# The second mixture of a two-layer perceiver: seven of eight tiles by blocks, one own block per expert

## The chip, the cores and the metric

The kernel runs on one core of a Trainium2 chip. The metric is the device time of one execution in microseconds (us). A core has five engines that run their own instruction streams in order: TensorE (PE, matrix products; its weight loads are listed as PEld), VectorE (DVE), ScalarE (ACT), GpSimd (POOL) and SyncE (SP, which only issues transfers here). Sixteen DMA engines move data between HBM and the on-chip memory. Everything is float32.

## The reference

Sixteen sequences of 64 tokens of width 256 (x, 1024 tokens, eight tiles of 128) and a context of 1601 rows per sequence pass two layers. Layer 0 has an attention with gathered samples, a self attention and a mixture of 8 experts. Layer 1 has a cross attention to the context, a state-space scan and a mixture of 32 experts. The last two parts are the ones that matter here:

```python
x = x + xattn1(layernorm(x), context)
x = x + attn1(layernorm(x))      # in projection, causal convolution of 4 taps, silu,
                                 # scan h = dA * h + dt * B * x over 16 states, gate, out projection
x = x + ffn1(layernorm(x))

def ffn1(x, ...):                                   # TOPK = 4, E = 32 experts, H = 128, HS = 512
    scores = softmax(flat @ router_w.T + router_bias)
    topk_scores, topk_idx = top_k(scores, TOPK)
    topk_scores = topk_scores / max(topk_scores.sum(-1), 1e-12)
    h = silu(einsum('nd,ehd->neh', flat, gate_w)) * einsum('nd,ehd->neh', flat, up_w)
    expert_out = einsum('neh,edh->ned', h, down_w)
    out = (take(expert_out, topk_idx) * topk_scores).sum(1)
    return out + silu(flat @ sgate_w.T) * (flat @ sup_w.T) @ sdown_w.T
```

Each token needs four of the 32 experts and all of the shared part, which is as large as four experts.

## The kernel before

PE, DVE and ACT follow an order that is written out by hand: Python generators yield between pieces of work, and a loop steps a main generator and a side generator in turn, so what is emitted first runs first on each of these engines. SP and POOL take their instructions in the order in which a scheduler places them, near the order of the program.

The cross attention (`Cross.step`) runs 128 steps, one for a sequence and a pair of heads, and three more that empty its pipeline. Since a tile is two sequences, tile t is complete after step 16(t + 1) + 3. While it runs, side work is stepped in it: layer 0's second half, and from step 56 on layer 1's state space (`Ssm.group`) and routing (`Route.group`) of the tiles that are complete. A group is two tiles. `Ssm.group` has a prelude (layer norm, input projection, convolution, step sizes), 16 scan steps over 128x512 elements (db, hs, hc on DVE, an add on POOL) and an output projection. `Route.group` writes a tile's mask, gates and normed rows (to `xnd` in HBM). Three groups run so; two tiles are left, whose sequences finish last.

After the third group comes `Table.slots`, still beside the cross attention. It turns the masks of six tiles into blocks of 128 rows, each for one expert: the tokens of each expert are counted and their counts rounded up to whole blocks, 6 * 128 * 4 slots and at most 127 rows of padding per expert, so 55 blocks at most (`NBA`). It computes each token's slot, each block's expert (`evr`) and each block's list of rows (`row`). The list is a sum of 48 small products (hb, hp) on PE, built in 8 parts of three tiles on DVE.

Then the cross attention's memory is given back, and the tail begins, in this order:

1. `dense(first, ...)`: the shared part of the six tiles, four parts of 128 hidden units, each in two chunks of 384 columns. Beside it `Ssm.group` of the last two tiles starts.
2. `sparse`: 55 blocks. `fetch` issues a block's gather of rows (POOL), reads its expert number into a register (SP) and loads that expert's weights (SP, 256 and 128 KB; 8 and 9 buffers, five blocks ahead). `turn` transposes the rows, `hidden` makes the hidden units, `down` the output, which ACT's queue writes to `ygd` in HBM two blocks at a time. Every second block steps the state space.
3. `dense(last, ...)`: the last two tiles, after their norm and routing, through the four shared parts and all 32 experts, each weighted by its gate, which is zero where the expert wasn't chosen. Every expert's weights are loaded again. Beside it `combine` gathers, for each of six tiles and four choices, the rows of `ygd` (24 gathers on POOL) and adds them to the residual with their gates.
4. The output of the last two tiles is stored.

Lines of the profile: L1040 is the cross attention's product with the context, L87 all plain products (told apart by their tiles: `st<-qf,cT` scores, `st<-xta,wg` shared parts, `st<-xbt,wg` blocks, `st<-gt,wg` the dense last tiles), L1026 the cross attention's output projection, L630 to L635 the table's parts, L1273, L1275 and L1280 the scan step on DVE, L1281 its add on POOL, L1298 and L1299 the swiglu, L1365 the blocks' gathers, L652 the gathers of `combine`.

Of the kernel before, what the change touches and what calls it, by code (L numbers as in the profile page):

```python
# [17 lines left out]
P = 128  # L18
# [31 lines left out]
NG = 4  # L50
# [3 lines left out]
NTA = NPAIR - TG  # L54
NBA = (NTA * P * TOP1 + E1 * (P - 1)) // P

# [8 lines left out]
def perceiver_kernel(ctx: ExitStack, tc: tile.TileContext, a: dict, out: bass.AP):  # L65
# [471 lines left out]
    def blocks_of(nt, ne, top):  # L537
        return (nt * P * top + ne * (P - 1)) // P
# [4 lines left out]
    xnd, ygd = mk(dram, [NTA * P, D], "xnd"), mk(dram, [blocks_of(NTA, E1, TOP1) * P, D], "ygd")  # L543

    class Table:


        def __init__(self, pool, nt, ne, top):
            self.pool, self.nt, self.ne, self.top = pool, nt, ne, top
            self.nb = blocks_of(nt, ne, top)  # L550
# [16 lines left out]
        def floor(self, y):  # L567
            sh = list(y.shape)
            yi, yf = mk(self.pool, sh, "fli", I32, bufs=1), mk(self.pool, sh, "flf", bufs=1)
            nc.vector.tensor_copy(yi, y)  # L570
            nc.vector.tensor_copy(yf, yi)
            nc.vector.tensor_tensor(y, yf, y, ALU.is_gt)
            nc.vector.tensor_tensor(y, yf, y, ALU.subtract)

        def slots(self):

            rp, on, nt, ne, nb, top = self.pool, self.on, self.nt, self.ne, self.nb, self.top
            n = nt * ne
            sh = [P, nt, ne]
# [4 lines left out]
            pos = mk(rp, sh, "pos", bufs=1)  # L584
            nc.vector.tensor_copy(pos.rearrange("p t e -> p (t e)"), pc)
            run_ = mk(rp, [P, nt + 1, ne], "run", bufs=1)
# [5 lines left out]
            own, end, base = (mk(rp, [P, ne], t, bufs=1) for t in ("nb", "end", "base"))  # L592
            nc.vector.tensor_scalar(own, run_[:, nt, :], float(P - 1), 1.0 / P, ALU.add, ALU.mult)
            self.floor(own)
            nc.vector.tensor_tensor_scan(end, on[:, :ne], own, 0.0, ALU.mult, ALU.add)
            nc.vector.tensor_tensor(base, end, own, ALU.subtract)
            nc.vector.scalar_tensor_tensor(pos, base.unsqueeze(1).to_broadcast(sh), float(P), pos, ALU.mult, ALU.add)
            sl, bk, self.w = (mk(rp, [P, top, nt], t, bufs=1) for t in ("slf", "bk", "gk"))
            tmp = mk(rp, sh, "tmp", bufs=1)
# [5 lines left out]
            tk, cf = mk(rp, [P, nt], "tokf", bufs=1), mk(rp, [P, P], "colf", bufs=1)  # L605
            nc.vector.tensor_copy(tk, self.tok)
            nc.vector.tensor_copy(cf, self.col)
            nc.vector.tensor_scalar(end, end, tk[:, :1], None, ALU.is_le)
            ev = mk(rp, [P, 1], "ev", bufs=1)
# [4 lines left out]
            nc.tensor.matmul(pe[:1, :nb], lhsT=ev[:nb], rhs=ident[:nb, :nb], start=True, stop=True)  # L614
# [3 lines left out]
            self.floor(bk)  # L618
            nc.vector.scalar_tensor_tensor(sl, bk, -float(P), sl, ALU.mult, ALU.add)
            self.expert = mk(rp, [1, nb], "evr", I32, bufs=1)  # L620
            nc.vector.tensor_copy(self.expert, pe[:1, :nb])
# [3 lines left out]
            half = nt // 2  # L625
            s1, s2 = [P, half, P], [P, half, nb]
            for q in range(2 * top):
                k, t = q // 2, slice(q % 2 * half, (q % 2 + 1) * half)
                hp, hb = mk(rp, s1, "hp", bufs=1), mk(rp, s2, "hb", bufs=1)
# [4 lines left out]
                for i in range(half):  # L634
                    nc.tensor.matmul(po, lhsT=hp[:, i, :], rhs=hb[:, i, :], start=q + i == 0, stop=q + i == 2 * top + half - 2)  # L635
# [531 lines left out]
    rows_d = [mk(dram, [NR, TOK], f"rows{g}") for g in range(NG)]  # L1167

    class Ssm:
# [15 lines left out]
        def group(self, g, wide=None):  # L1185
# [3 lines left out]
            tiles = range(g * TG, (g + 1) * TG)  # L1189
            sh = [P, KC, TOK]  # L1190
            xn = normed(tiles, "m", mp)
            yield
            xt = turned(xn, TG, "m", mp)
            yield
            xpad = mk(mp, [P, KC, NS2, S + NCONV - 1], "xpad")
            nc.gpsimd.memset(xpad[:, :, :, : NCONV - 1], 0.0)
            zs = mk(mp, sh, "zs")
            for e in range(2 * KC):
                pz = bank()[:, :TOK]
# [14 lines left out]
            pp = bank()[:NR, :TOK]  # L1214
            mm(pp, [(w_xp[:, c, :], xc[:, c, :]) for c in range(KC)])
            prm = mk(mp, [NR, TOK], "prm")
            nc.scalar.copy(prm, pp)
            nc.sync.dma_start(out=rows_d[g], in_=prm)

            def spread(r0, n, tag, bufs, pool=mp):  # L1220

                t = mk(pool, [P, n, TOK], tag, bufs=bufs)
                nc.sync.dma_start(out=t, in_=rows_d[g][r0 : r0 + n, :].unsqueeze(0).to_broadcast([P, n, TOK]))
                return t
# [63 lines left out]
            for t in range(TG):  # L1288
                po = bank()
                mm(po[:, :D], [(y[:, c, t * P : (t + 1) * P], w_out[:, c, :]) for c in range(KC)])  # L1290
                nc.vector.tensor_tensor(x4[:, g * TG + t, :], po[:, :D], x4[:, g * TG + t, :], ALU.add)
# [9 lines left out]
    class Route:  # L1301
        def __init__(self, rp, mp):
# [3 lines left out]
            self.tb = Table(rp, NTA, E1, TOP1)  # L1306
# [29 lines left out]
        def group(self, g):  # L1336
            xn = normed(range(g * TG, (g + 1) * TG), "m", self.mp)
            nc.sync.dma_start(out=xnd[g * TOK : (g + 1) * TOK, :].rearrange("(t p) d -> p t d", p=P), in_=xn)
            yield
            xt = self.xt[:, :, g * TOK : (g + 1) * TOK]  # L1340
            tp = transposes([xn[:, t, k * P : (k + 1) * P] for k in range(KC) for t in range(TG)])
            nc.scalar.copy(xt.rearrange("p k (t n) -> p k t n", n=P), tp.rearrange("p (k t) n -> p k t n", t=TG))
            yield
            for t in range(TG):
                j = g * TG + t
# [4 lines left out]
    def sparse(ep, tb):  # L1350

        AHEAD = 5
        xb, yb = {}, {}
        st = {}

        def fetch(i):

            if i >= tb.nb:
                return
            if i % 4 == 0:  # L1360
                m = min(4, tb.nb - i)
                st["ev"] = mk(ep, [1, 4], "ev4", I32, bufs=3)
                nc.vector.tensor_copy(st["ev"][:, :m], tb.expert[:, i : i + m])
            x = mk(ep, [P, D], "xb", bufs=6)
            nc.gpsimd.indirect_dma_start(  # L1365
                out=x, out_offset=None, in_=xnd, in_offset=bass.IndirectOffsetOnAxis(ap=tb.row[:, i : i + 1], axis=0)
            )
            v = nc.sync.value_load(st["ev"][0:1, i % 4 : i % 4 + 1], min_val=0, max_val=E1 - 1)
            wg = mk(ep, [P, KC, 2, HID1], "wg", bufs=8)
            wd = mk(ep, [P, D], "wd", bufs=9)  # L1370
            nc.sync.dma_start(out=wg, in_=a["guT"][bass.ds(v, 1)].rearrange("o (k p) i h -> p (o k) i h", p=P))
            nc.sync.dma_start(out=wd, in_=a["down1T"][bass.ds(v, 1)].rearrange("o h d -> (o h) d"))
            xb[i] = (x, wg, wd)

        def turn(i):
            if i >= tb.nb:
                return
            x, wg, wd = xb.pop(i)
            tp = transposes([x[:, k * P : (k + 1) * P] for k in range(KC)])
            xt = mk(ep, [P, KC, P], "xbt", bufs=3)  # L1380
            nc.scalar.copy(xt, tp[:, :KC, :])
            st[i] = (xt, wg, wd)

        def hidden(i):
            xt, wg, wd = st.pop(i)
            ph = big()[:, : 2 * P].rearrange("p (i n) -> p i n", i=2)
            for h in range(2):
                mm(ph[:, h, :], [(wg[:, k, h, :], xt[:, k, :]) for k in range(KC)])
# [315 lines left out]
```

## Time and profile before

| | |
|---|---|
| median of 6 runs | 3376.29 us (3369.82 to 3392.59) |
| the profiled execution | 3371.39 us |
| its span, first to last instruction | 3369.6 us |
| mean granted PE clock | 0.943 of full |
| PE busy | 2949.9 us (88% of the span) |
| PE weight loads | 2416.8 us (72%) |
| DVE busy | 1619.0 us (48%) |
| ACT busy | 1012.8 us (30%) |
| POOL busy | 808.6 us (24%) |
| HBM read and written | 248.90 MB and 74.22 MB |

The shares are means over stages that are limited by different things; the tail, from the end of the cross attention at about 3075 us on, is a small piece of the span. Matmuls of float32 stand in the trace as two instructions each. In the views, a line of a group gives engine, operation, out<-in, shapes and count, then busy time and mean duration in ns, then the idle time of the engine just before these instructions with what ended it. The chain of waits lists start, duration and what ran, back from the last instruction. A timeline line gives start, duration, engine, line, operation and in brackets the idle time before it.

### The profile page before, as it was taken

The numbers are of one execution on the slowest core, as the hardware profiler recorded it, in microseconds if no ns is written. First come the engines' busy times: TensorE is split into PE (matmuls) and PEld (weight loads), VectorE is DVE, ScalarE is ACT, GpSimd is POOL, SyncE is SP. The second block draws the span as 40 slices with busy tenths as digits, with TensorE's granted clock in tenths as the row PEclk, the third lists the DMA queues.
The fourth block names the chain that finished last, engine by engine and source line by source line (L and its number), as shares of the span: only waits on it lengthen the run. The fifth ranks groups of instructions, "written<-read, shape, count | busy, mean of one in ns | idle before, by whom it ended". The sixth has DMA issues, their size and how long they took to land.

```text
span 3369.6 us, 46371 instructions
## 1 busy us (share of the span) xinstructions
PE 2949.9 (88%) x17710; PEld 2416.8 (72%) x17710; DVE 1619.0 (48%) x4126; ACT 1012.8 (30%) x2353; POOL 808.6 (24%) x919
## 2 busy tenths in 40 slices
PE   6779988893778888879889999999999999999879
PEld 3444444562667777778778999999989999997766
DVE  4311113223434444545554334676568568665846
ACT  2233333331121221222332333333244343222421
POOL 0354334545423333432000001010002002000721
PEclk8889998996888889989999999999999999999989
DMA  6377664562320111011213541121112112103884
GB/s 192 110 150 158 210 174 139 172 198 56 109 75 25 43 40 56 24 55 41 67 40 97 171 135 55 47 80 55 48 35 80 49 54 74 35 1 108 257 231 123
DMA packets 338710, 326.19 MB, mean 97 GB/s; under 512 B 59301, under 2 KB 289097, under 8 KB 337977
## 3 DMA queue, kind: packets, MB, share of 16 engines
q1 hardware_dynamic: 186473, 226.04, 21.7%
q10 hardware_dynamic: 126640, 62.79, 6.8%
q0 software_dynamic: 25376, 34.39, 4.5%
q8 instruction: 141, 2.31, 0.3%
q14 instruction: 80, 0.66, 0.1%
HBM read 248.90 MB, written 74.22 MB: 96 GB/s over the span
## 4 chain that ended last, share of the span: by engine, by line
PE 75%; DVE 10%; another core or an unknown queue 6%; issue 4%; ACT 3%; DMA 2%; POOL 0%; SPq 0%; ACTq 0%; DVEq 0%
PE st L87 31%; PE mm L1040 19%; PE mm L87 15%; PE mm L152 5%; PE mm L996 2%; DMA wg<-in_guT 1%; PE mm L1026 1%; PE mm L965 1%; DVE hs L1275 1%; ACT pt L1110 0%; PE mm L1088 0%; DVE mp L1071 0%; PE mm L1098 0%; DVE cv L471 0%
## 5 line engine op out<-in xcount | busy, mean ns | idle before, releaser
L427 POOL DMA_INDIRECT g<-tab,ig x640 | 610.7, 954 | 893.5 <-DVE ig L425 695.2
L87 PE MATMUL st<-qf,cT 128*128 128x128 f32 x6144 | 762.0, 282 | 50.2 <-ACT qf L999 33.2
L87 PEld LDWEIGHTS st<-qf,cT 128*128 128x128 f32 x6144 | 739.0, 198 | 59.0 <-ACT qf L999 37.2
L1040 PE MATMUL mm<-cn,pt 128*128 128x257 f32 (+1 forms) x3072 | 758.1, 391 | 0.7 <-ACT cT L81 0.7
L1040 PEld LDWEIGHTS mm<-cn,pt 128*128 128x128 f32 (+1 forms) x3072 | 565.6, 194 | 87.7 <-issue 2.0
L87 PE MATMUL st<-wkv,cxt 128*128 128x512 f32 (+1 forms) x832 | 397.1, 623 | 24.3 <-ACT kv L380 14.9
L1071 DVE TENSOR_REDUCE mp<-st 128x128 f32<-128x512 f32 x384 | 260.5, 688 | 266.7 <-PE st L87 216.5
L1109 DVE TENSOR_TENSOR pt<-st,mc 128x512 f32<-128x512 f32 (+1 forms) x384 | 224.0, 639 | 165.5 <-ACT mc L1100 148.9
L87 PEld LDWEIGHTS st<-wkv,cxt 128*128 128x128 f32 (+1 forms) x832 | 156.6, 198 | 194.0 <-issue 169.4
L1110 ACT ACTIVATE pt<-pt 128x512 f32<-128x512 f32 (+1 forms) x384 | 207.3, 588 | 58.0 <-DVE pt L1109 55.9
L380 ACT COPY kv<-st 128x512 f32<-128x512 f32 (+1 forms) x208 | 119.7, 590 | 239.1 <-PE st L87 155.5
L1100 ACT COPY mc<-mm 128x128 f32<-128x128 f32 x128 | 34.1, 267 | 410.2 <-PE mm L1098 321.5
L1090 DVE TENSOR_REDUCE xmx<-mm 128x1 f32<-128x128 f32 x128 | 37.3, 292 | 243.6 <-PE mm L1088 200.9
L1049 ACT COPY ot<-mm 128x256 f32<-128x256 f32 x128 | 47.5, 371 | 345.5 <-PE mm L152 312.8
L459 DVE TENSOR_REDUCE smx<-sc 128x4 f32<-128x20 f32 x32 | 5.4, 168 | 287.3 <-ACT sc L457 286.7
L87 PE MATMUL mm<-xt,w 128*128 128x256 f32 x512 | 121.4, 391 | 5.5 <-DVE act L815 5.5
L87 PEld LDWEIGHTS mm<-xt,w 128*128 128x128 f32 x512 | 99.8, 196 | 30.0 <-issue 9.0
L1281 POOL TENSOR_TENSOR ys<-ys,hc 128x512 f32<-128x512 f32 x64 | 81.6, 1275 | 161.0 <-DVE hc L1280 160.8
L1365 POOL DMA_INDIRECT xb<-xnd,row x55 | 54.7, 994 | 241.0 <-PE mm L1026 199.8
L1016 ACT COPY yt<-mm 128x64 f32<-128x64 f32 x128 | 27.3, 213 | 272.1 <-PE mm L87 239.4
L87 PE MATMUL mm<-w,act 128*128 128x256 f32 x256 | 71.3, 420 | 40.4 <-DVE x L795 26.5
L87 PE MATMUL mm<-ot,wvi 128*64 128x64 f32 x1024 | 75.1, 227 | 25.7 <-ACT ot L1049 25.7
(441 smaller groups left out, 3891.9 us busy)
## 6 DMA issues: line engine op xcount, KB each, us to landing
tab<-kv ACTq DMA_DIRECT2D x48, 1024.0 KB
w<-in_gate SPq DMA_DIRECT2D x62, 512.0 KB
cx<-in_ctx SPq DMA_DIRECT2D x48, 512.0 KB
cn<-in_ctx SPq DMA_DIRECT2D x16, 1408.0 KB
wg<-in_guT SPq DMA_DIRECT2D x87, 256.0 KB
wk<-in_xwkiT SPq DMA_DIRECT2D x32, 512.0 KB
w<-in_lin SPq DMA_DIRECT2D x31, 512.0 KB
wd<-in_down1T SPq DMA_DIRECT2D x87, 128.0 KB
```

What stands on the lines that cost most here:

```text
L87: nc.tensor.matmul(o, lhsT=l, rhs=r, start=i == 0, stop=i == len(pairs) - 1)
L152: nc.tensor.transpose(t[:ncol, i, :rows], b, ident[:rows, :rows])
L380: nc.scalar.copy(kv[:w, :, c, :], pk[:w].rearrange("p (h e) -> p h e", h=H0))
L427: nc.gpsimd.indirect_dma_start(out=gf[:, (half * n + s) * 4 * HD0 : (half * n + s + 1) * 4 * HD0], out_offset=None, in_=tables[j], in_offs ...
L996: nc.tensor.matmul(pf[:, k * P : (k + 1) * P], lhsT=w[:, hp % 4, k * P : (k + 1) * P], rhs=rhs, start=True, stop=True)
L1040: nc.tensor.matmul(po, lhsT=pt[:w, c, :], rhs=cn[:w, c, :], start=c == 0, stop=c == NCH - 1)
L1049: nc.scalar.copy(ot, tp[:, :KC, :])
L1071: nc.vector.tensor_reduce(mp_[:, i, :], s.rearrange("p c n -> p n c"), AX.X, ALU.max)
L1109: nc.vector.tensor_tensor(o, st[i][:, :m, :], mc.to_broadcast([P, m, P]), ALU.subtract)
L1110: nc.scalar.activation(o, o, AF.Exp)
L1281: nc.gpsimd.tensor_tensor(y, y, hc, ALU.add)
L1365: nc.gpsimd.indirect_dma_start(out=x, out_offset=None, in_=xnd, in_offset=bass.IndirectOffsetOnAxis(ap=tb.row[:, i : i + 1], axis=0))
```

## The change

- Seven tiles go by blocks and one stays dense (`NTA`).
- In this table (`own=True`) every expert has one block of its own, block e for expert e, for its first 128 tokens; tokens beyond go to further blocks whose expert is found at run time. That gives 32 + 27 = 59 blocks.
- `Table.slots` is run after the cross attention, three steps after each chunk of the shared parts. Its list of rows is built in 12 parts (3, 3 and 1 tiles for each of four choices).
- The state space and routing run beside the cross attention for groups at tiles 0, 2, 4 (two tiles) and 6 (one tile), two side steps per step, three for the one-tile group. After the cross attention one tile is left (128x256 elements per scan step).
- One of the four shared weights is loaded during the cross attention (`EARLY`); weight buffers go from 8 and 9 to 15 and 16.
- The shared parts of seven tiles take three chunks per part (384, 384, 128).
- The 27 further blocks come first, with a step of the state space in each. The 32 own blocks follow, interleaved with the last tile's 32 experts, which use the same weights in memory: 59 loads of an expert's weights where there were 55 + 32.
- The last tile's shared parts come after its experts. `combine` (28 gathers) starts when the last own block is done, two adds per dense part that is left.

```diff
-NTA = NPAIR - TG
-NBA = (NTA * P * TOP1 + E1 * (P - 1)) // P
+NTA = NPAIR - 1
+EARLY, WB = 1, 15
...
+        return ne + (nt * P * top - top) // P if own else (nt * P * top + ne * (P - 1)) // P
...
+            if self.own:
+                nc.vector.tensor_scalar(more, run_[:, nt, :], -1.0, 0.0, ALU.add, ALU.max)
+                nc.vector.tensor_scalar(more, more, 1.0 / P, None, ALU.mult)
...
+                q_, o_ = mk(tp, sh, "tmp", bufs=1), mk(tp, sh, "flf", bufs=1)
+                nc.vector.tensor_scalar(q_, pos, float(P), None, ALU.is_ge)
+                nc.vector.tensor_tensor(o_, q_, base.unsqueeze(1).to_broadcast(sh), ALU.mult)
+                nc.vector.tensor_tensor(o_, o_, cf[:, :ne].unsqueeze(1).to_broadcast(sh), ALU.add)
+                nc.vector.scalar_tensor_tensor(pos, o_, float(P), pos, ALU.mult, ALU.add)
...
-            half = nt // 2
-            for q in range(2 * top):
+            w = 3 if self.own else 2
+            parts = [(k, t, min(w, nt - t)) for k in range(top) for t in range(0, nt, w)]
+            for q, (k, t, n) in enumerate(parts):
+                hp, hb = mk(tp, [P, w, P], "hp", bufs=1)[:, :n], mk(tp, [P, w, nb], "hb", bufs=1)[:, :n]
...
+    class Blocks:
+        def step(self):
+            n = self.n
+            if n > len(self.order):
+                return False
+            self.n += 1
+            if n == 0:
+                self.fetch(self.ahead)
+                self.turn(0)
+            if n < len(self.order):
+                self.fetch(n + 1 + self.ahead)
+                self.turn(n + 1)
+                i = self.order[n]
...
+                swiglu(act, sl, ph[:, 0, :], ph[:, 1, :])
+                self.d[i] = (act, wd)
+            self.down(n - 1)
+            return True
...
-        for g in range(NG - 1):
-            side = chain([ssm.begin] * (g == 0) + [ssm.group(g), rt.group(g)] + [rt.tb.slots] * (g == NG - 2))
+        for t0 in (0, TG, 2 * TG, 3 * TG):
+            nt = min(TG, NTA - t0)
+            side = chain([ssm.begin] * (t0 == 0) + [ssm.group(t0, nt), rt.group(t0, nt)])
...
+                cr.step(side, side)
+                if nt == 1:
+                    next(side, None)
...
+        table = chain([side, lambda: rt.tb.slots(ep)])
+        side = ssm.group(NTA, NPAIR - NTA, ep)
+        more = Blocks(ep, rt.tb, range(E1, rt.tb.nb), 5)
+        own = Blocks(ep, rt.tb, range(E1), 4)
+        run(side, 4)
+        for i, _ in enumerate(dense(first, ep, rt.xt, shared)):
+            if table.gi_frame:
+                run(table, 3)
+            else:
+                more.fetch(5)
                 next(side, None)
+        while more.step():
+            next(side, None)
+            if more.n == len(more.order) - 2:
+                own.fetch(4)
         drain(side)
+
         xn = normed(last, "g", ep)
+        own.step()
         xt = turned(xn, NPAIR - NTA, "g", ep)
...
+        own.step()
+        for t in range(NPAIR - NTA):
+            for _ in rt.scores(xt, t, mask, gw[:, t, :]):
+                own.step()
+        shared = [(e, lambda e=e: weights(ep, e)) for e in parts]
+        late = dense(last, ep, xt, [(e, lambda e=e: own.w[e]) for e in range(E1)] + shared, gw)
...
-        dense(last, ep, xt, range(-(HS1 // P), E1), side, gw, routers)
+        for e in range(E1 + len(shared)):
+            next(late)
+            if own.n <= E1:
+                own.step()
+                if e % 4 == 3:
+                    own.step()
+            else:
+                run(side, 2)
+        drain(late)
         drain(side)
```

## The prediction

> **What bounds the kernel now.** I read first the stages (busy time per window), then the chain of waits, then the timeline and the groups of VectorE for single prices.
>
> ```profile
> 3000.00:3050.00 50.00, 50.00 (x377) 46.15 (x376) 28.17 (x68) 12.02 (x32) 0.00 (x0) 1.00 0.00 1
> 3100.00:3150.00 50.00, 41.90 (x220) 31.91 (x218) 46.99 (x96) 18.61 (x54) 24.30 (x31) 0.97 0.67 219
> 3150.00:3200.00 50.00, 43.22 (x290) 36.51 (x291) 38.50 (x92) 23.27 (x74) 35.14 (x40) 1.00 1.00 300
> 3200.00:3250.00 50.00, 35.13 (x226) 30.85 (x224) 16.57 (x59) 15.13 (x48) 11.12 (x12) 0.90 0.95 251
> 3300.00:3370.00 70.00, 62.86 (x263) 47.69 (x261) 41.83 (x104) 8.23 (x22) 5.65 (x6) 0.98 0.35 106
> ```
>
> Columns: window, length, busy us of PE, weight load, DVE, ACT, POOL, then granted clock, DMA share, GB/s. Up to 3050 the cross attention keeps PE full. Then the limits change every 50 us: DVE (46.99 of 50), the DMA engines (1.00 and 0.95), and PE again in the dense last stage. So the change must be priced stage by stage. The chain of waits says what ends last in each:
>
> ```profile
> 2996.77 3.63 PE st L87 x32
> ...
> 3009.82 0.61 PE mm L635 x6
> 3010.43 3.63 PE st L87 x32
> ...
> 3037.15 3.57 PE st L87 x32
> ...
> 3049.48 3.57 PE st L87 x32
> ```
>
> One step of the cross attention is 12.33 us bare (3037.15 to 3049.48) and 13.66 us with two parts of the table (`slots`, L635) in it.
>
> ```profile
> 3176.34 1.24 DVE hs L1275
> 3180.53 1.23 DVE hs L1275
> ...
> 3221.17 10.84 DMA wg<-in_guT
> ...
> 3298.88 1.73 PE st L87 x8
> 3301.75 1.73 PE st L87 x8
> ```
>
> Beside the state space two blocks take 4.1 to 4.2 us (one scan step between), set by DVE; then the weights' arrival decides; in the end PE, at 2.88 us per expert of two tiles.
>
> **The change, stage by stage.** The tail of before runs from the last cross projection's end (3075.6) to 3369.6: 294.0 us, made of 9.5 (prelude of the state space) + 37 (shared parts, to 3122) + 126 (55 blocks) + 6 + 111 (36 dense parts) + 4.6.
>
> *Cross attention.* Removed: the table. Its steps (numbers 120 to 125) exceed the bare ones by 0.6 + 0.7 + 1.33 + 1.33 + 1.34 + 0.7 = 6.0 us. Added: one tile of state space and routing. A group of two tiles costs about 8 us here: 3.5 and 2.3 us in the two steps that hold its prelude (PE waits for DVE's convolution at 2458.7 to 2462.4), 1.7 where it ends, the rest spread; its 16 scan steps cost nothing (12.33 with two in a step), because PE covers them. One tile: between half (4) and all (8) of it; I take 4.5, near half, since rows of 128x256 halve. Net -1.5, bounds -2 to +3. The 384 KB loaded early hide behind DMA that is 0 to 20% busy there; without that cover about 1.5 us.
>
> *A, prelude.* One layer norm (0.42 + 0.18 + 0.41 us) and half of the 5.4 us of input projection fall away: 9.5 becomes 5.3.
>
> *B, shared parts with the table.* PE: a chunk of 384 takes 2.6, of 128 0.9 (four products of a block, below), a tile's second product 0.43: 4 x (2 x 2.6 + 0.9 + 7 x 0.43) = 36.4. The table adds 28 products of 0.2 and 3 small: 8. DVE prices:
>
> ```profile
> L630 DVE TENSOR_TENSOR hp<-colf,slf 128x384 f32<-128x384 f32 x8 | 4.4, 556 | 1.0 <-PE mm L635 1.0
> L632 DVE TENSOR_TENSOR hb<-hb,tokf 128x165 f32<-128x165 f32 x8 | 2.7, 332 | 0.3
> L601 DVE SCALAR_TENSOR_TENSOR tmp<-rank,pos 128x192 f32<-128x192 f32 x4 | 1.4, 358 | 0.1
> ```
>
> A build of three tiles is hp + hb + hb = 1.36 us with 0.04 between instructions; there are 8 of these and 4 of 0.75 for single tiles: 13.9. The 224-wide rows scale 0.36 to 0.41 (22 of them: 10 us), some 30 small ones of 0.2: 6. Table 30 us; swiglu 8 x 1.18 + 4 x 0.62 = 12; adds 4 x 2.5 = 10; state space prelude 8. DVE 60, PE 45. But they don't overlap, since both orders are written out. After each chunk PE holds the products of two builds, and hp and hb have one buffer: build (1.36), products (0.85), build (1.36), products, next chunk (2.6), tanh and swiglu (0.9 after it), and only then the next build. Chunks 0 to 1 with positions and slots end at 18 us; chunk 2 and its builds at 23; chunk 3 with the second product (3.0) at 34.7; 4 at 43; 5 at 50; 6 with the second product and the last products at 56; the list of rows is out at 57, the gate weights at 61, so the first expert numbers reach SP at 62; chunks 7 to 11 with two second products, each waiting for DVE, at 76.5. That is at full clock. The clock:
>
> ```profile
> 3206.13 1.13 PE L87 MATMUL st<-xbt,wg 128*128 128x128 f32 x8 [1.63 <-DMA wg<-in_guT]
> 3209.93 2.01 PE L87 MATMUL st<-xbt,wg 128*128 128x128 f32 x8 [2.01 <-DMA wg<-in_guT]
> 3253.54 0.94 POOL L652 DMA_INDIRECT yk<-ygd,sli  x1 [24.27 <-DMA wg<-in_guT]
> 3254.79 0.95 POOL L652 DMA_INDIRECT yk<-ygd,sli  x1 [0.30 <-issue]
> ```
>
> After 2.0 us of idle the same products took 2.01 instead of 1.13. PE is 70% busy at clock 0.90 in 3200 to 3250; here it would be 55 to 60% busy with pauses of 1.4 to 2.5 us. At a mean clock of 0.8 the same chain is 85, at 0.6 it is 101. I take 84, bounds 76 and 101.
> [...]
>
> *C, 27 blocks beside one tile of state space.* Now there is a scan step in every block. DVE: swiglu 0.62, half a copy 0.21, db, scan, hc at half of 0.70, 1.23, 0.69 plus a start of 0.07 (0.42, 0.64, 0.42), gaps: 2.4 us, over PE's 1.55 (3238.67 to 3240.22 in the timeline). 16 x 2.4 + 1 of 2 + 10 x 1.55 + 2 at the start = 58. A block moves 640 KB, 2.2 us at 300 GB/s, 2.6 at 251: covered by the 2.4, and a lead of five blocks covers most of the last ten. Bounds 55 and 66 (all at 2.45). POOL: gather 1.25 + add 0.64 (half of the 1.276 of L1281) + memset 0.13, under 2.4. On SP the four loads of the state space's rows (2 MB) stand among the first weights and delay those by up to 7 us; the first block starts 14 us after its weights are asked for, which covers it.
>
> *D, one tile's norm and routing.* Before 6 us until its first product, now under four own blocks (6.2 of PE) in the same in-order queues: 9, bounds 7 and 12.
>
> *E, own blocks with the last tile's experts.* 28 more blocks of 1.55 and 24 experts of 1.33 (a block without its two transposes, 0.22) = 75.3; waits, 78. Blocks need 2.7 us each here, the DMA 2.2 to 2.6, so the loads just fit; at the 219 GB/s of the slowest slices of the DMA view inside this stretch they would be 84. SP issues 59 expert loads where it issued 87; the 15 buffers let it run ahead.
>
> *F, the combination.* It needs every block's output, the last of which is written now only at the end of E. Copy and issue 0.8, landing 3 (2.2 at 2026, 4.4 at 3249 under load), 28 gathers on POOL at 1.25 us (0.95 + 0.30) = 35, the last one's landing 1.9, add 0.5, output 3.6 (3366.05 to 3369.6): 45. The 12 dense parts left are 16 us of PE and hide in it. Before, the 24 gathers hid in 111 us of dense work; that cover is gone and about 29 us stick out.
>
> Sum: 5.3 + 84 + 58 + 9 + 78 + 45 = 279.3 against 294.0; with the cross attention -16. The profiled execution's own time is 3371.4, so 3355; it lies 4.9 under the median of the six runs, so 3360 as a median.
>
> **Rivals.** (1) *The table stalls the shared stage at half clock.* For: a one-buffer ping-pong of PE and DVE, and the 2.01 us row. Against: PE is still over half busy. B at clock 0.5 is 114, so 3390: slower. It decides from B = 110. (2) *The loads bound blocks and experts.* Fetching starts only 66 us into the tail of after; 59 blocks and 2 MB of state-space rows are 40.7 MB, at 235 GB/s 173 us, E's end 10 us later: 3370, no change. For: 251 GB/s with PE waiting at 3221. Against: 300 GB/s at 3150, and E's slower need. (3) *Table and chunks overlap after all*, B is DVE's 60: 3336. Against: the written order. That weights are not shared is excluded: the changed order of instructions has one load per expert.
>
> **How the numbers follow.** Forecast 0.55, (1) 0.13, (2) 0.18, (3) 0.14. What can be told from no change is 0.3%, 10 us: faster is under 3366. Forecast's own range 3347 to 3372 (B 76 to 92, the others by a few us); with (2) whole and parts of (1) and (3) the range is 3336 to 3390. A quarter of the forecast lies over 3366. Faster: 0.14 + 0.41 = 0.55; same: that quarter and (2) but for a little, 0.28; slower: (1) and the rest, 0.17.
>
> **What would show it.** In the new profile: bare 12.33 us steps to the end of the cross attention; about 80 us between the first product of the shared parts and the first block, with DVE and PE alternately idle at hp and the products of L655; 2.4 us per block for 16 blocks, then 1.6; 3.2 us per own block and expert; 45 us with POOL at 1.25 us per gather at the end, PE idle for 25 of them. B over 110 or E over 100 would make me wrong.

## The result and the profile after

The changed kernel takes 3400.2 us, median of 20 runs (3383.02 to 3412.18); the kernel before, run beside it, 3379.91 us, median of 46. The ratio is 1.0058, 95% interval [1.0045, 1.0072]: slower by 20 us, where 16 us less were forecast. The profiled execution has a span of 3395.4 us against 3369.6.

The windows of the changed kernel, with the columns of before:

```profile
3100.00:3150.00 50.00, 32.08 (x114) 23.52 (x113) 27.70 (x90) 5.17 (x12) 0.00 (x0) 0.70 0.05 16
3150.00:3200.00 50.00, 40.45 (x181) 30.52 (x181) 31.45 (x86) 10.42 (x30) 14.50 (x19) 0.85 0.51 138
3200.00:3250.00 50.00, 37.43 (x258) 32.05 (x256) 39.93 (x100) 22.57 (x75) 33.80 (x49) 1.00 0.98 262
3350.00:3396.00 46.00, 19.25 (x94) 15.68 (x94) 21.86 (x61) 2.50 (x9) 24.22 (x26) 0.75 0.33 98
```

In the first two windows, the shared parts with the table, no engine is near full, and the clock is 0.70 and 0.85; the DMA engines are busy for 0.05 of the first and 0.51 of the second, which reaches into the blocks. In the third, the blocks, the DMA engines are full at 0.98. In the last, the combination, PE is busy 19 of 46 us.

The chain of waits of the changed kernel:

```profile
3052.56 3.57 PE st L87 x32
...
3124.00 1.53 PE mm L655 x6
3125.54 5.23 PE st L87 x8
...
3202.11 0.86 DVE db L1295
...
3246.93 5.71 DMA wg<-in_guT
...
3357.51 4.75 another core or an unknown queue
```

The table's products (L655, before L635) now stand alone in the chain, and a chunk that took 2.74 us in the kernel before (at 3085.06, clock 1.00) takes 5.23. In the blocks the chain goes through `db`, one of the two shorter products of the scan step on VectorE, then through a weight load, and in the combination through something that the profile cannot name.

The stages, measured in the traces between the same instructions (us). "43-53" and "54-126" are steps of the cross attention; "empty" is from the start of step 127 to the end of the last projection; "blocks" reaches to the last tile's norm, which is 4.4 us behind the 27th block in the changed kernel (2.8 to 9.2 in the others); "comb." starts at the last own block's product.

| run | 43-53 | 54-126 | empty | A | B | blocks | own, experts | comb. | ratio to before |
|---|---|---|---|---|---|---|---|---|---|
| before | 245.9 | 1011.4 | 26.3 | 9.5 | 37.0 | - | - | - | |
| changed | 253.3 | 1015.1 | 31.6 | 6.4 | 86.0 | 73.2 | 81.4 | 52.0 | 1.0058 |
| after_again | 253.3 | 1015.1 | 31.6 | 6.5 | 85.9 | 73.2 | 81.4 | 48.5 | 1.0057 |
| after_third | 253.2 | 1015.5 | 31.5 | 6.7 | 83.7 | 72.6 | 82.3 | 44.0 | 1.0039 |
| b_two_buffers | 253.4 | 1015.0 | 31.6 | 6.5 | 79.3 | 72.7 | 81.5 | 52.4 | 1.0040 |
| b_late_products | 253.4 | 1015.1 | 31.6 | 6.5 | 60.6 | 74.5 | 81.5 | 52.4 | 0.9986 |
| c_no_pool_add | 253.4 | 1015.1 | 31.6 | 6.6 | 85.5 | 72.6 | 81.7 | 48.9 | 1.0065 |
| c_early_weights | 253.3 | 1015.1 | 31.6 | 6.5 | 84.2 | 76.2 | 82.2 | 43.8 | 1.0035 |
| c_more_only | 253.3 | 1013.4 | 32.8 | 6.0 | 85.9 | 74.4 | 81.3 | 48.5 | 1.0056 |
| c_stores_sync | 253.3 | 1015.1 | 31.6 | 6.5 | 84.2 | 68.2 | 81.3 | 43.7 | 1.0013 |
| c_more_stores_sync | 253.3 | 1015.0 | 31.6 | 6.4 | 84.4 | 65.9 | 80.6 | 43.6 | 1.0006 |
| x_pace_of_before | 253.3 | 1011.8 | 40.0 | 9.2 | 85.8 | 72.6 | 81.2 | 48.2 | 1.0073 |
| x_four_steps | 253.3 | 1029.4 | 26.3 | 5.1 | 83.1 | 72.8 | 82.4 | 43.8 | 1.0037, one run |
| v3_again | 253.2 | 1015.1 | 31.6 | 6.4 | 59.1 | 66.8 | 77.9 | 44.0 | 0.9921 |

The kernel before took 3352 to 3388 us on some chips and 3083 to 3088 on others; ratios are always against runs of the kernel before on the same chip. The difference lies in the code ahead of step 54, which both kernels run, and, for the changed kernel, in the combination; for one and the same kernel the stages between agree within 3 us.

### The profile page after: what moved, and what is told of

It is laid out like the page before. It is cut to its first block, busy times and chain, and to the rows that moved or that the text cites. A ratio compares the mean times of both kernels' runs of the same rounds, so it can differ in the third digit from the quotient of the medians.

```text
span 3395.4 us, 46368 instructions
## 1 busy us (share of the span) xinstructions
PE 2933.8 (86%) x17754; PEld 2414.6 (71%) x17754; DVE 1624.9 (48%) x4213; ACT 1025.8 (30%) x2413; POOL 821.4 (24%) x960
## 4 chain that ended last, share of the span: by engine, by line
PE 74%; DVE 11%; another core or an unknown queue 6%; issue 4%; ACT 3%; DMA 1%; POOL 1%; ACTq 0%; DVEq 0%; SPq 0%; POOLq 0%
PE st L87 31%; PE mm L1060 19%; PE mm L87 15%; PE mm L152 5%; PE mm L1016 1%; PE mm L1046 1%; PE mm L985 1%; DVE hs L1297 1%; PE mm L1108 0%; DVE mp L1091 0%; DVE pt L1129 0%; ACT pt L1130 0%; DVE db L1295 0%; POOL g L427 0%
## 5 line engine op out<-in xcount | busy, mean ns | idle before, releaser
L427 POOL DMA_INDIRECT g<-tab,ig x640 | 610.0, 953 | 900.6 <-DVE ig L425 703.2
L87 PE MATMUL st<-qf,cT 128*128 128x128 f32 x6144 | 759.7, 281 | 48.3 <-ACT qf L1019 29.9
L1091 DVE TENSOR_REDUCE mp<-st 128x128 f32<-128x512 f32 x384 | 259.4, 687 | 253.2 <-PE st L87 207.7
L1303 POOL TENSOR_TENSOR ys<-ys,hc 128x512 f32<-128x512 f32 (+1 forms) x80 | 84.8, 1059 | 184.9 <-DVE hc L1302 184.6
```

The source lines that it names most:

```text
L87: nc.tensor.matmul(o, lhsT=l, rhs=r, start=i == 0, stop=i == len(pairs) - 1)
L427: nc.gpsimd.indirect_dma_start(out=gf[:, (half * n + s) * 4 * HD0 : (half * n + s + 1) * 4 * HD0], out_offset=None, in_=tables[j], in_offs ...
L1091: nc.vector.tensor_reduce(mp_[:, i, :], s.rearrange("p c n -> p n c"), AX.X, ALU.max)
L1303: nc.gpsimd.tensor_tensor(y, y, hc, ALU.add)
```

## The experiments

### The shared parts with the table (B)

Three builds of the one-hot tiles (`hp`, `hb`) on VectorE and their products on TensorE follow each chunk. The timeline of the changed kernel, VectorE and TensorE, from one round:

```profile
3152.65 0.56 DVE L650 TENSOR_TENSOR hp<-colf,slf 128x384 f32<-128x384 f32 x1
3153.90 1.54 PE L655 MATMUL mm<-hb,hp 128*128 128x59 f32 x6 [1.28 <-DVE hb L652]
3155.47 0.56 DVE L650 TENSOR_TENSOR hp<-colf,slf 128x384 f32<-128x384 f32 x1 [1.63 <-PE mm L655]
3156.72 1.54 PE L655 MATMUL mm<-hb,hp 128*128 128x59 f32 x6 [1.28 <-DVE hb L652]
3158.04 4.48 PE L87 MATMUL st<-xta,wg 128*128 128x384 f32 x8
```

The brackets answer each other: TensorE waits 1.28 us for `hb`, VectorE 1.63 us for the product that frees `hp`. Two edits test it. The first gives two buffers:

```diff
-hp, hb = mk(tp, [P, w, P], "hp", bufs=1)[:, :n], mk(tp, [P, w, nb], "hb", bufs=1)[:, :n]
+hp, hb = mk(tp, [P, w, P], "hp", bufs=1 + self.own)[:, :n], mk(tp, [P, w, nb], "hb", bufs=1 + self.own)[:, :n]
```

> The one-hot tiles hp and hb of the table get two buffers each after the cross attention; nothing else changes. Theory (the one buffer makes VectorE and TensorE take turns): in the changed kernel builds follow each other every 2.82 us (hp at 3152.65 and 3155.47) though one takes 1.36 of VectorE. With two buffers the second build of a round follows the first at once, a round of three gets 2 us shorter, four rounds 8: the stage from the first shared product to the first block goes from 86.0 to about 78, the whole by -8 (ratio to the kernel before 1.0035). Rival (the written order: TensorE's next chunk stands behind the products of the last build anyway, and the clock stays halved): 84 to 86, nothing on the whole.

B took 79.3 us, as the theory has it. The ratio, 1.004 [1.002, 1.006], overlaps that of the changed kernel, so it is the stage that shows the gain. The second moves the products (`lag` is 3 in this table; after the loop the rest is issued):

```diff
-hp, hb = mk(tp, [P, w, P], "hp", bufs=1)[:, :n], mk(tp, [P, w, nb], "hb", bufs=1)[:, :n]
+hp, hb = mk(tp, [P, w, P], "hp", bufs=lag + 1)[:, :n], mk(tp, [P, w, nb], "hb", bufs=lag + 1)[:, :n]
...
+held.append((q, n, hp, hb))
+if len(held) > lag > 0:
+    product()
 yield
```

> The products of the three builds of a round are issued a round later, behind the next chunk of the shared parts, with four buffers of hp and hb; the amount of work is the same. Theory (the stage is long because the written order makes TensorE and VectorE take turns, which also halves the clock): VectorE is busy 54 of the 86 us, TensorE 50 at that low clock; overlapped, the stage takes 60 to 68 us, the whole -18 to -26, ratio about 0.999. Rival (it is long because of the amount of work, or the clock stays low whatever the order): 80 or more, ratio above 1.004.

B took 60.6 us, ratio 0.9986 [0.9971, 1.0]. The timeline of that kernel, TensorE:

```profile
3108.23 1.67 PE L652 MATMUL mm<-hb,hp 128*128 128x59 f32 x14
3109.73 2.80 PE L87 MATMUL st<-xta,wg 128*128 128x384 f32 x8
3112.37 1.67 PE L652 MATMUL mm<-hb,hp 128*128 128x59 f32 x14
```

All products of a round run in one piece and without a wait, and the chunk takes 2.80 us in place of 4.48 to 5.44. The windows over the stage show the clock, first the changed kernel, then this one:

```profile
3103.00:3145.00 42.00, 26.95 (x88) 18.66 (x87) 22.82 (x77) 3.21 (x9) 0.00 (x0) 0.71 0.01 2
3145.00:3189.00 44.00, 33.13 (x135) 24.19 (x133) 25.78 (x70) 4.43 (x10) 6.67 (x7) 0.84 0.34 92
```

```profile
3085.00:3115.00 30.00, 21.74 (x100) 16.18 (x98) 24.55 (x84) 4.19 (x11) 0.00 (x0) 0.87 0.03 10
3115.00:3146.00 31.00, 26.53 (x122) 19.13 (x122) 23.33 (x67) 4.14 (x9) 6.65 (x7) 0.97 0.46 115
```

VectorE does the same 48 us of work in both. TensorE's busy time falls from 60.1 to 48.3 us for the same products, as its clock rises, and its idle time in the stage from 26 to 13 us. So 25 of B's 86 us came from the written order, about 12 of them as clock and 13 as waits.

### The blocks (C)

The prediction counted 2.4 us for a block beside a scan step. The trace has 2.63 (16 `db` from 3194.43 to 3233.87). GpSimd's sum and VectorE's `db` in the changed kernel:

```profile
3201.93 0.73 POOL L1303 TENSOR_TENSOR ys<-ys,hc 128x256 f32<-128x256 f32 x1
3202.03 0.93 DVE L1295 TENSOR_TENSOR db<-dx,pb 128x256 f32<-128x256 f32 x1
...
3204.55 0.73 POOL L1303 TENSOR_TENSOR ys<-ys,hc 128x256 f32<-128x256 f32 x1
...
3204.98 0.60 DVE L1295 TENSOR_TENSOR db<-dx,pb 128x256 f32<-128x256 f32 x1
```

Both times `db` ends 0.30 us after GpSimd's add (3202.96 against 3202.66, 3205.58 against 3205.28), whenever it began. The edit leaves that add out for the last tile (`wide` is set there alone):

```diff
-nc.gpsimd.tensor_tensor(y, y, hc, ALU.add)
+if wide is None:
+    nc.gpsimd.tensor_tensor(y, y, hc, ALU.add)
```

> The running sum of the last tile's state space (y += hc, 16 on GpSimd) is left out, so that tile's output is not the reference's; all else is as in the changed kernel. Theory (VectorE's db is slowed while GpSimd works on SBUF beside it): db takes 0.42 to 0.48 us in every block in place of 0.93 in every second and 0.60 in others, a block beside a scan step 2.3 to 2.4 us in place of 2.63, the stage of the blocks 64 to 65 in place of 68.8. Rival (the loads of the weights slow it): db stays at 0.93, the pitch at 2.6.

The timeline of that kernel:

```profile
3174.75 0.42 DVE L1295 TENSOR_TENSOR db<-dx,pb 128x256 f32<-128x256 f32 x1
...
3176.86 0.42 DVE L1295 TENSOR_TENSOR db<-dx,pb 128x256 f32<-128x256 f32 x1
```

All 16 `db` took 0.41 to 0.42 us and a block 2.42: the theory holds for `db`, and 2.4 was right without GpSimd. But the stage stayed at 72.6 us: what VectorE gave up was lost again at its end. The next edits ask what ends it. `ask` is `fetch` without the gather:

```diff
 run(table, 3)
+if hasattr(rt.tb, "expert"):
+    more.ask(12)
...
 while more.step():
     next(side, None)
+    more.ask(more.n + 12)
+    own.ask(more.n + 13 - len(more.order))
```

> The weights of the first 12 of the 27 blocks are asked for as soon as the list of experts is known (after some 16 us of the shared parts, where the DMA engines stand at 0.05) and the lead stays 12; the own blocks' weights follow as buffers come free. Theory (the arrival of weights sets the end of the block stage, which is why a shorter scan step gave nothing): the stage of the blocks up to the last tile's norm goes from 73.2 to 64 to 66 us (16 of 2.66, 11 of 1.55, start and end), the rest unchanged: -8 on the whole. Rival (the loads only move: they slow the shared parts or come up short among the own blocks): the shared stage 88 or more, or own blocks with experts 88 in place of 81, nothing on the whole.

76.2 us, ratio 1.0035 [1.002, 1.005]: the rival's outcome. In its trace ScalarE waited 3 us for a store of `yb`, with the DMA engines at 0.95 to 1.00. Without the last line of the edit:

> As c_early_weights, but the own blocks' weights are asked for where the changed kernel asks for them, at the end of the 27 blocks. Theory (in c_early_weights the block stage kept its length because the own blocks' 13 weights were then loaded in it: DMA share 1.00, and ScalarE, in order, waited 3 us for yb's store with the next blocks' copies behind it): with 12 of the 27 weights loaded beforehand and nothing else added, the stage of the blocks takes 64 to 67 us in place of 73.2, own blocks with experts 81 to 84, the whole -7: ratio 1.001 where c_early_weights had 1.0035. Rival (the stage is set by something other than the loads): 72 or more, ratio 1.0035.

74.4 us, ratio 1.0056 [1.0038, 1.0074]: a miss again. With 12 weights asked for ahead of time the stage should not wait for a load, and yet it did. The 27th block was done 67.0 us into the stage; then ScalarE's first step of the last tile's norm waited for a load that it does not read (engine, line, releaser: total us, times, longest):

```profile
ACT L98 <- DMA wd<-in_down1T: 4.5, 1, 4.5
```

The changed kernel's own timeline has the clue, between the 26th block and the 27th:

```profile
3248.15 0.37 ACT L81 COPY yb<-mm 128x256 f32<-128x256 f32 x1 [0.16 <-PE mm L87]
...
3249.06 0.60 PE L87 MATMUL mm<-wd,bact 128*128 128x256 f32 x2
...
3252.73 0.37 ACTq L1436 DMA_DIRECT2D ygd<-yb  x1
3253.14 0.37 ACT L1422 COPY xbt<-mm 128x256 f32<-128x256 f32 x1 [4.62 <-DMA wg<-in_guT]
...
3253.56 2.08 PE L87 MATMUL st<-xbt,wg 128*128 128x128 f32 x8 [3.91 <-ACT xbt L1422]
```

TensorE waits for a copy on ScalarE (`xbt`), whose input was ready at 3248.3; ScalarE stands in front of the store of the outputs, which it issues at 3252.73 only, though the last copy that the store reads (`yb`) ended at 3248.52. The trace puts the wait of 4.62 us down to a load of weights, which neither the copy nor the store reads. That the store stood behind this load, and the next block's copy behind the store, was the author's reading: no trace shows what the store waited for. If this wait ends the stage, 73.2 us less 4.6 leave 68.6; the author's estimate was 68 to 70. The edit:

```diff
-nc.scalar.dma_start(
+nc.sync.dma_start(
     out=ygd[(i + 1 - m) * P : (i + 1) * P, :].rearrange("(n p) d -> p n d", p=P), in_=self.y[:, :m, :]
 )
```

> The changed kernel with the stores of the blocks' outputs (ygd) issued by SyncE in place of ScalarE; nothing else. [...] Rival (the loads themselves are late, whoever waits for them): 72 to 74, nothing on the whole.

68.2 us, ratio 1.0013 [1.0002, 1.0024] where the changed kernel itself has 1.0039 [1.0024, 1.0053] (after_third): as estimated. In the list of waits for this stage ScalarE's copy `xbt` no longer waits for a load, and TensorE's weight load waits 1.6 us in place of 7.1 for `xbt`; first the changed kernel, then this one:

```profile
PEld st L87 <- ACT xbt L1422: 7.1, 3, 4.3
...
ACT xbt L1422 <- DMA wg<-in_guT: 4.6, 1, 4.6
```

```profile
PEld st L87 <- ACT xbt L1422: 1.6, 1, 1.6
```

Now the early weights as well, for the 64 to 67 us that were expected of c_more_only:

> c_more_only with the stores on SyncE. [...] Rival (the DMA engines, at 0.97 to 1.03 there, are the bound: a block moves 640 KB of weights, 128 gathered and 128 stored): 71 or more.

65.9 us, ratio 1.0006 [0.9996, 1.0015]. With 12 weights asked for ahead of time the stores on ScalarE cost 8.5 us (74.4 against 65.9), without them 5.0 (73.2 against 68.2). So, of the stage's excess over the forecast, 5.0 us came from stores on ScalarE (4.4 against after_third), 2.3 from weights asked for late, and 3 to 4 are left. No wait for a load in the list of this kernel is longer than 0.2 us, so loads don't explain what is left. GpSimd's add beside `db` would: 16 blocks of 2.61 us here, in place of 2.4, make 3.4 us. That is reckoned and not shown, since no run leaves out the add with the stores moved.

### The cross attention

Two edits on the pace of the side work. The first undoes the change's pace for the first group:

```diff
-cr.step(side, side)
+cr.step(side if t0 or cr.n % 2 else None, side)
```

> The first group's state space beside the cross attention is paced as in the kernel before (every second step gives one part less). Theory (two parts in each step make TensorE wait for VectorE where the group's prelude stands): steps 57 to 61 of the cross attention take 73 us in place of 77.8, the whole -4.7. Rival (the wait comes back where the group then ends later): the steps after 61 get longer by as much, nothing on the whole.

Each came true in part. Steps 54 to 126 were 3.3 us shorter, and steps 57 to 61 took 73.1 us, as the theory has it; but then the seventh tile, two steps later, cost 8.4 us more while the pipeline empties and 2.8 in A. Ratio 1.0073 [1.0044, 1.0101]. The second gives the seventh tile four parts per step:

```diff
-    next(side, None)
+    run(side, 2)
```

> The seventh tile's state space gives four parts in each step of the cross attention in place of three, so that its norm and routing come before the pipeline is emptied. Theory (they cost 5.3 us there because TensorE waits for the norm and then runs at half clock): the emptying takes 26 to 28 us in place of 31.6, steps 122 to 126 stay at 12.3. Rival (VectorE has no room for a fourth part): those steps take 13 or more, nothing on the whole.

The emptying fell to 26.3 us, as before the change, but steps 122 and 123, with four scan steps, took 13.1 us each and the three behind them 18.8, 17.0 and 14.0: steps 54 to 126 came to 14.3 us more. The seventh tile's norm and routing cost more beside the full pipeline than in its emptying. What they cost in the emptying is seen in the changed kernel, first, with the kernel before under it:

```profile
3081.00 0.44 PE L152 MATMUL mm<-ident,mn 128*128 128x128 f32 x2 [3.37 <-DVE mn L102]
...
3082.68 3.60 PE L1060 MATMUL mm<-cn,pt 128*128 128x257 f32 x8
```

```profile
3064.07 5.49 PE L1040 MATMUL mm<-cn,pt 128*128 128x257 f32 x24
```

TensorE waits 3.37 us for the norm, then eight products take 3.60 us; before, 24 of them took 5.49 in one piece.

### The combination

The three pauses of VectorE in the changed kernel:

```profile
3362.28 0.48 DVE L1483 SCALAR_TENSOR_TENSOR x<-mm,gw,x 128x256 f32<-128x256 f32 x1 [4.77 <-remote]
...
3368.02 0.48 DVE L1483 SCALAR_TENSOR_TENSOR x<-mm,gw,x 128x256 f32<-128x256 f32 x1 [3.95 <-remote]
...
3383.26 0.42 DVE L1479 TENSOR_TENSOR x<-mm,x 128x256 f32<-128x256 f32 x1 [4.55 <-remote]
```

The product that the first one reads ended at 3356.5; what it waited for after that the trace doesn't name. `f_direct_loads` takes the gathers of the last combination away:

```diff
-nc.gpsimd.indirect_dma_start(
-    out=y, out_offset=None, in_=yd,
-    in_offset=bass.IndirectOffsetOnAxis(ap=tb.slot[:, k, t : t + 1], axis=0),
-)
+nc.sync.dma_start(out=y, in_=yd[i * P : (i + 1) * P, :])
```

> The 28 gathers of the combination (indirect, issued by GpSimd) become plain loads of as many bytes issued by SyncE, so its sums are of other rows than the reference's. Theory (the pauses of VectorE and ScalarE in the combination, 4 to 10 us each, come with the dense sequence of gathers): no pause over 2.5 us after the first landing, the stretch from the last own block's product to the end takes 28 to 32 us in place of 52. Rival (the pauses belong to the place in the instruction stream, whatever moves the data): VectorE still pauses 3 to 6 us at about 28 and 12 us of work before the end; 38 or more.

29.2 us and no pause. But the other kernels run on that chip, with all their gathers, had no pause either, and a combination of 43.8: so this run shows what the gathers' pitch costs, 14.6 us, and not what the pauses are. So the two kernels were run again as they are:

> The changed kernel itself, on the chip of this call. Theory (the pauses without a releaser belong to the chip, not to the kernel: the profiles of the second call have none anywhere, those of the first call and of the result have some 70, and in the combination they cost 8 us): if the head here has none, the combination takes 43.8 us and the ratio is 1.003 to 1.0045; if the head has them, 48 to 52 us and 1.005 to 1.0065. Rival (they belong to the kernel's gathers): 52 us and 1.0058 on any chip.

1.0057 [1.0026, 1.0088], with 73 pauses without a releaser, 48.5 us.

> The changed kernel on this call's chip: 1.003 to 1.004 where the profile shows no pauses without a releaser (c_stores_sync, 5 us shorter, had 1.0013 on such a chip), 1.0057 where it does.

1.0039 [1.0024, 1.0053], no such pause in the whole span, 44.0 us. The timeline of after_third, VectorE, in the combination:

```profile
3060.37 0.48 DVE L1483 SCALAR_TENSOR_TENSOR x<-mm,gw,x 128x256 f32<-128x256 f32 x1
3060.76 0.28 DVE L1320 SCALAR_TENSOR_TENSOR sl<-sl,st 128x128 f32<-128x128 f32 x1
...
3062.58 0.48 DVE L683 SCALAR_TENSOR_TENSOR x<-yk,gk,x 128x256 f32<-128x256 f32 x1 [0.82 <-DMA yk<-ygd,sli]
```

There it waits for the gathers alone. The kernel before, on a chip with pauses:

> The kernel before itself, on the chip of this call. Its tail from the end of the last cross projection was 294.0 us and had no pause without a releaser. Theory: 292 to 295 here too, whatever the head takes; emptying 26.3. Rival (its stages differ from chip to chip as the head does): a tail outside 290 to 298.

68 pauses, all ahead of 1567 us; its tail was 293.5 us (3089.0 to 3382.5). The emptying took 27.9 us where 26.3 were expected, so 1.6 us is how far that stage scatters in one kernel. Since the same program has pauses on some chips and none on others, they belong to the chip or its condition at the time and not to the gathers alone.

They do go with the gathers, though. In all ten profiles that have pauses (64 to 83 each, 280 to 375 us in sum), every one falls in the run of layer 0's 640 gathers on GpSimd (L427, from about 115 to 1526 to 1576 us), most of which start 0.3 us after the one before, or among the 28 gathers of the changed kernel's combination, which also follow one another without a break. The gathers of the blocks, some 2.6 us apart, and those of the combination before, mostly 2.9 us apart, have none. So a dense series of gathers looks like a condition, and the changed kernel put one at the end of its span. That is a coincidence in time and no test: neither `f_direct_loads` nor a kernel with its gathers further apart was run on a chip with pauses, and what the pauses are stays open.

### Versions

> The late products, the early weights, and the copies of the 27 blocks' outputs all on ScalarE. Theory: the shared stage 61 us, a block beside a scan step 2.45 (2.66 less half a copy of 0.42), the stage of the blocks 61, in all 37 less than the changed kernel: ratio 0.995 to the kernel before. Rival (the loads are the bound, so a shorter shared stage leaves them less time): the block stage 72 or more, ratio 0.999 or above.

Ratio 0.996 [0.9948, 0.9972], B 59.1, blocks 73.3: the late products pay, the rest not. The copies on ScalarE gained nothing, since `db` then met GpSimd's add in every block (0.81 to 0.94).

> The late products, the early weights of c_more_only, and an additional own block after every third expert in place of every fourth, so that the own blocks end two experts earlier. Theory: shared stage 60 us, blocks 65, own blocks with experts 79, combination 44 without pauses: 42 less than the changed kernel, ratio 0.992. Rival (the loads take back what the shorter shared stage gives): blocks 72 or more, ratio 0.996 as v1_order_and_weights.

Ratio 0.9965 [0.9944, 0.9987], blocks 72.7, with pauses (combination 52.8).

> v2_all with the stores on SyncE. Theory: as v2_all with the block stage at 65 us in place of 72.7, ratio 0.993 to 0.9945. Rival (DMA engines as the bound): 71 or more, ratio 0.9965.

Ratio 0.9911 [0.989, 0.9931], blocks 66.8; and

> v3_all_stores again, on this call's chip: 0.989 to 0.993 where the profile shows no pauses, 0.992 to 0.995 where it does (8 us more in the combination).

0.9921 [0.9902, 0.994]. This version beats both kernels on a chip without pauses; with pauses it was not run. Does the kernel before gain by the stores alone?

> The kernel before with only the stores of its blocks' outputs moved from ScalarE to SyncE. [...] Rival (there the loads themselves are late, since the scan holds the pace and a wait for wg of 10.84 us stands in its chain): 126, ratio 1.000, so that v3's gain belongs to the changed kernel's design.

1.0008 [0.9998, 1.0018], its 55 blocks 123.5 us, against 126.0 and 124.7 in the two profiles of the kernel before: 1.2 to 2.5 us less, where the 27 blocks of the changed kernel gained 4.4 to 5.0, so nearer the rival. Its tail, 290.6 us, is 3 shorter than before in the one profile, which the ratio doesn't show. In the kernel before TensorE itself waits for the weights, and still does with the stores moved (first before, then this kernel):

```profile
PE st L87 <- DMA wg<-in_guT: 14.4, 8, 4.1
```

```profile
PE st L87 <- DMA wg<-in_guT: 13.4, 11, 1.7
```

v3's gain needs the changed design.

## Why the prediction was wrong

Two terms failed: the cross attention, put at -1.5 us, and the blocks (C), put at 58. Between the two profiles they account for 18 and 11 of the 42 us by which the forecast was off; the pauses in the combination, which were not priced, for 7.

*Cross attention, forecast -1.5, measured +16 from step 43 on.* (Step 42 is 1.7 us shorter in the changed kernel, so +15 with it.) TensorE runs the same 2582 matrix products from step 36 to 54 in both kernels, only in another order, so it isn't added work there. Three things. Steps 43 to 53, which the prediction did not look at because the first mixture seemed untouched, take 253.2 to 253.4 us in place of 245.1 to 245.9 in every profile: +7.4. `Table.slots` serves both mixtures, and it gained a `yield`, so the first mixture's parts stand one part later in the written order (the builds of its list move from steps 42 and 43 to 43 and 44). That reading was not tried by taking the `yield` out, so the cause of this part is argued and not shown. Steps 54 to 126 are +3.7 in place of -1.5: the pacing with two parts a step was not priced, and the pace of before takes 3.3 of it back (x_pace_of_before). The emptying is +5.3 and was put at nothing, since the seventh tile's norm and routing were not followed into it; with them moved ahead it takes 26.3 again (x_four_steps).

*A*, forecast 5.3, measured 6.4. *B*, forecast 84, measured 86.0: right as a number, and the alternation of builds and products is the mechanism given; the two edits show it. The parts are less good: VectorE was busy 48.6 us where 60 were counted. The bounds 76 and 101 stood on the clock, and it was 0.71 to 0.84. The prediction counted on pauses of 1.4 to 2.5 us, and that is wrong: while positions and slots are made, TensorE stands still for 8.24 us, and behind that the granted clock is 0.50. First the changed kernel's timeline, then its window; then two windows of b_late_products, which has the same pause:

```profile
3117.39 0.24 PE L634 MATMUL mm<-ident,ev 27*1 27x27 f32 x2 [8.24 <-DVE ev L631]
```

```profile
3114.00:3130.50 16.50, 10.26 (x30) 7.38 (x31) 7.59 (x29) 0.77 (x2) 0.00 (x0) 0.50 0.00 1
```

```profile
3096.50:3103.00 6.50, 2.91 (x12) 2.54 (x13) 5.25 (x21) 0.28 (x1) 0.00 (x0) 0.50 0.01 3
3103.50:3144.00 40.50, 38.02 (x186) 28.25 (x184) 31.46 (x86) 5.40 (x12) 6.65 (x7) 1.00 0.31 78
```

Behind the pause the changed kernel, with its alternation, has half clock for 16.5 us; the late products have it for 6.5 and then the full clock for 40. So the clock is down behind the long pause in both, and stays down for longer where builds and products alternate. There it also falls again, 20 us later in the timeline of the changed kernel:

```profile
3136.65 0.88 PE L655 MATMUL mm<-hb,hp 128*128 128x59 f32 x6 [2.67 <-DVE hb L652]
3138.81 1.53 PE L655 MATMUL mm<-hb,hp 128*128 128x59 f32 x6 [1.28 <-DVE hb L652]
```

The same six products take 0.88 us and then 1.53, after gaps of 2.67 and 1.28 us, and no longer gap lies between 3118 and there; the granted clock is 0.98 from 3130.5 to 3136 and 0.50 from 3138.5 to 3140.5. So it fell here with no gap above 2.67 us since it had risen, and the forecast was right to put B above the 76 us of the full clock.

*C*, forecast 58, measured 68.8 to the 27th block: the step that failed in the tail. The sum of VectorE's rows took `db` at half its former time and left GpSimd's add out of it: 2.63 us per block where 2.4 were counted, and 2.42 without the add. "A block moves 640 KB, covered by the 2.4" is right in its bytes (384 KB of weights, 128 gathered, 128 stored); what it left out is who waits for these transfers: ScalarE in front of a store cost 5.0 us, and late-asked weights 2.3. The lead of five blocks seemed to settle the row `DMA wg<-in_guT`. In the kernel before it stands for TensorE waiting for weights, and moving the stores left 13.4 of 14.4 us of that wait; in the changed kernel it stands for ScalarE in front of a store (one wait of 4.6 us, gone with the stores moved). In both rows above `db` ends 0.30 us after the add, which began first, and takes 0.93 and 0.60 us, where it took 0.41 to 0.42 without the add.

*D and E*, forecast 9 + 78, measured 85.9 from the 27th block to the last own block (4.4 and 81.4): right as a sum. *F*, forecast 45, measured 44.0 without pauses and 52.0 with: the pitch of 1.25 us per gather was right. The pauses were left out; the trace of before has 69, but none behind 1558 us, and only beside layer 0's gathers.

So the tail was forecast at 279.3 us and took 299.1 (289.4 in after_third, without pauses), against 294.0 before: a gain of 4.6 without pauses, a loss of 5 with them. Without pauses the kernel is still slower, 1.0039, since the cross attention loses more than the tail gains. The rest of the 25.8 us between the profiles, about 4, lies ahead of step 43, where executions of one kernel scatter by more than that (step 0 starts at 992.9 and 1002.3 in two profiles of the kernel before).

*The rivals.* (1) The stall at half clock came true only as far as priced in the forecast (86, not 110). (2) The loads did decide the end of the blocks, but mostly through ScalarE's waits in front of stores, which the trace puts down to loads (5.0 us by moving the stores, 2.3 by asking for weights earlier), and not in E. (3) B at 60 is what the late products reach; the written order alone kept it from that, as the argument against (3) said.

## What to carry to other kernels

Price a helper that the edit touches in every place that calls it, and price the emptying of a pipeline by itself. Ask which queue issues a store: here ScalarE stood 4.62 us with a store in front of its next copy, and with the stores in SyncE's queue (c_stores_sync) the blocks took 5.0 us less. The sign was a copy that waits "for a DMA" whose data it does not read. Where two engines alternate by a written order, issue the consumer one round late; here that alone was worth 25 us of 86.

## What the runs showed of the hardware

VectorE's two-input product of 128x256 took 0.42 us alone and 0.93 with GpSimd's add begun 0.1 us before. TensorE went from 0.88 to 1.53 us for six products, at a granted clock of 0.50 in the second, with pauses of 2.67 and 1.28 us, 0.9 us of work between them. ScalarE stood 4.62 us ahead of a copy for a weight load that the copy doesn't read, with a store in front of the copy; with the stores moved to SyncE no copy `xbt` waited for a load. The same two kernels took some 300 us less on some chips than on others, nearly all of it ahead of step 54. On the quicker ones it was 845 to 851 us to the first step and 902 to 912 for steps 0 to 53, and no pause without a known releaser; on the others 975 to 1009 and 1039 to 1057, with 64 to 83 such pauses, all of them beside a dense series of gathers on GpSimd.
